# Packed queries and keys made into tiles by masking on ScalarE instead of transfers, with GpSimd and the transfer queue in program order

## The chip, the cores and the metric

The kernel runs on one core of one Trainium2 chip. A core has a matrix engine (TensorE, PE in the profile), three engines for elementwise work (VectorE or DVE, ScalarE or ACT, GpSimd or POOL), a queue that mostly issues transfers (SyncE or SP), and 16 DMA engines which move data between the device memory and the on-chip memory (SBUF). Matrix products land in PSUM[...]. The metric is device time in microseconds (us) of one execution; several runs are taken and their median is given.

## The reference

The input is x, 2 sequences of 2048 tokens with 256 features, in float32. Six blocks are added to it in turn, each on a layer normalization of x:

```python
x = x + 0.5 * L0_ffn(layernorm(x))    # mixture of 6 experts, the best 2 of each token, and a shared one
x = x + L0_attn(layernorm(x))         # 16 heads of 16, every key, q scaled by 1/16
x = x + 0.5 * L0_ffn(layernorm(x))    # the same experts again
x = x + 0.5 * L1_ffn(layernorm(x))    # a gated recurrence of two steps, then a product and tanh
x = x + L1_attn(layernorm(x))         # 16 heads, causal, rotary, relative positions within 32
x = x + 0.5 * L1_ffn(layernorm(x))
```

The first attention is softmax(q k^T) v per head, and an output product with a bias. The second turns q and k by rotary tables (pairs of features, cos and sin of the position), scales q by 1/4, adds to each score the product of q with a learned vector that depends on the distance of key and query, clipped to 32, masks keys that come later, and adds to the weighted values the learned vectors weighted in the same way.

## The kernel before

**Layout and stages.** x stays in SBUF as 32 chunks of 128 tokens; `Norm` (L91 to L120) makes statistics (`stat`, L91/92, DVE), the reciprocal root (`root`, L96 to L98, GpSimd), the normalized tokens (`normal`, L109), and their transposes (`turn`, PE L119, ScalarE L120). By the trace of before, the stages run one after the other: MoE 1 to about 350 us, attention 0 to about 2101, MoE 2 to about 2430, a recurrence to 2628, attention 1 to 3978, and the second recurrence with the output to 4169.

**MoE.** Tokens are sorted by expert into the DRAM buffer `places`, in two halves of 37 tiles of 128 rows. `experts` (L350 to L414) loops over the tiles of one half: load of `xs` (L366), transposes (L369), up product (L376), silu and product (L381, L383), transposes (L388), down product (L395), store to `results` (L402). `combine` (L418 to L428) fetches by GpSimd's indirect transfers (`yg`, L423) the two results of each token of a chunk, and adds them on DVE (L428). The 16 chunks of the second half come at the end of the stage.

**Heads in a tile.** A group is 4 heads at 512 queries. Its queries and keys lie in tiles of 128 partitions, 32 to a head: 16 rows of features, one row in which the keys hold 1 and the queries hold minus the row's maximum, and zeros. A product with a 128-wide piece of the weights gives 128 dense feature rows, that is two groups. ScalarE copies it from PSUM to a tile `packed`, and `spread` brings its rows to the two tiles by eight transfers of 16 rows each on SP's queue. Keys' remaining rows come from a DRAM array `pads` by further transfers (`pad_keys`); queries' tiles are cleared by GpSimd.

**Attention 0** works in units; 16 make a group. In each, PE forms four score products of queries x keys for the maximum (L715, DVE L719), four transposed products (L727), whose exponentials ScalarE takes (L732), and the four weighted sums of the unit before (L739). The result goes through ScalarE (`gather`, L605) to a sum on GpSimd (L610). When a group's maxima are there, `subtract` (L596 to L600) puts their negatives into the queries' tile. Queries are made (L701 to L709) every second group, keys (L680 to L692) and values (L578, L584) of the first sequence before the first unit, those of the second along the way; `divide` (L619 to L623) and `outputs` (L642) end a group and a block.

**Attention 1** has the same pieces under a schedule of steps of two units: for each group n, maxima run in steps `Ms` to `Me`, exponentials in `Es` to `Ee`, and queries come `early`. `rotate` (L961 to L976) does the rotary work: a copy to SBUF (ScalarE), a shuffle (DVE L969) and three operations on GpSimd (L971 to L975). `by_position` (L1019) multiplies queries by the 32 distance vectors; the result is skewed into a diagonal band by a store to DRAM on ScalarE's own queue (`skew<-s`, L1026) and a load (`band_load`, L1036, `band<-skew`, 1.28 MB). `largest` (L1059 to L1097) joins it to the scores (L1083) and finds the maxima, and GpSimd subtracts them from the band (L1097). After use the band goes to DRAM (`band_store`, L1105, `pd<-band`) and comes back by diagonals (`positions_load`, L1182) for the distance vectors' part of the result (`positions_exp`, `positions_T`, `positions`, L1190 to L1201). The schedule is written at L1205 to L1283. Transfers and masks go out in a list `sends`, in half steps.

**Order of work.** Instructions of PE, ScalarE and DVE are issued in program order everywhere (`ENGINES`, L156). SP's, and in the attentions GpSimd's, are placed by a planner, which orders them by its own estimate of times; in MoE and recurrence GpSimd too has program order. Each engine takes its instructions in order, so one that waits holds up those behind it.

```python
def spread(dst, src, i):
    for j in range(J):
        nc.sync.dma_start(out=dst[32 * j : 32 * j + DH], in_=src[ds(64 * i + DH * j, DH), :])
```

Of the kernel before, what the change touches and what calls it, by code (L numbers as in the profile page):

```python
# [10 lines left out]
F32 = mybir.dt.float32  # L11
# [6 lines left out]
P = 128  # L18
# [24 lines left out]
def macaron_kernel(ctx: ExitStack, tc: tile.TileContext, t: dict, out: bass.AP):  # L43
# [8 lines left out]

    xpool = ctx.enter_context(tc.tile_pool(name="xpool", bufs=1))
# [3 lines left out]
    for b in range(NTB):  # L57
        nc.sync.dma_start(out=x[:, ts(b, CPB), :], in_=x_in[:, ts(b, CPB), :])

# [71 lines left out]
    def spread(dst, src, i):  # L131

        for j in range(J):
            nc.sync.dma_start(
                out=dst[32 * j : 32 * j + DH], in_=src[ds(64 * i + DH * j, DH), :]
            )

    def pad_keys(dst):
        n = dst.shape[-1]
        for j in range(J):  # L140
            nc.sync.dma_start(out=dst[32 * j + DH : 32 * j + 32], in_=t["pads"][j, :, 0:n])
# [14 lines left out]
    ENGINES = {mybir.EngineType.PE, mybir.EngineType.Activation, mybir.EngineType.DVE}  # L156
# [9 lines left out]
    def moe(w, ws, gate_w, gate_b, rev, tri, iota, z, behind, last, gathered):  # L166
# [3 lines left out]
        with ExitStack() as s:  # L170
# [179 lines left out]
            def experts(h, exi, between):  # L350

                xT, h_, hT, val = {}, {}, {}, {}
                GROUP = 8

                def tile_in(i):
                    if i % GROUP == 0:
                        n = min(GROUP, NST - i)
                        _, vs = nc.values_load_multi_w_load_instructions(
                            exi[0:1, i : i + n], engines=[mybir.EngineType.PE],
                            min_val=0, max_val=(NE - 1) * EW,  # L360
                            skip_runtime_bounds_check_because="a sum of five comparisons times EW",
                        )
                        for k, v_ in enumerate(vs):
                            val[i + k] = v_
                    xs = wk.tile([P, D], F32, name="xs", bufs=4)
                    nc.sync.dma_start(out=xs, in_=places[h][ts(i, P), :])  # L366
                    pt = bank()
                    for kc in range(2):
                        nc.tensor.transpose(pt[:, ts(kc, P)], xs[:, ts(kc, P)], ident)  # L369
                    xT[i] = wk.tile([P, D], F32, name="xT")  # L370
                    nc.scalar.copy(xT[i], pt[:, 0:D])  # L371

                def up(i):
                    pu = bank()
                    for kc in range(2):
                        nc.tensor.matmul(  # L376
                            pu, lhsT=xT[i][:, ts(kc, P)], rhs=w[:, kc, ds(val[i], 2 * D)],
# [4 lines left out]
                    h_[i] = wk.tile([P, D], F32, name="h")  # L382
                    nc.vector.tensor_tensor(h_[i], sg, pu[:, D:], ALU.mult)  # L383

                def turn(i):
                    ph = bank()
                    for kc in range(2):
                        nc.tensor.transpose(ph[:, ts(kc, P)], h_[i][:, ts(kc, P)], ident)  # L388
                    hT[i] = wk.tile([P, D], F32, name="hT")
                    nc.vector.tensor_copy(hT[i], ph[:, 0:D])  # L390

                def down(i):
                    po = bank()
                    for kc in range(2):
                        nc.tensor.matmul(  # L395
                            po[:, 0:D], lhsT=hT[i][:, ts(kc, P)],
                            rhs=w[:, kc, ds(val[i] + 2 * D, D)],
# [5 lines left out]

                tile_in(0)
                for i in range(NST + 2):
                    between(i)
                    if i + 1 < NST:
                        tile_in(i + 1)
                    if i < NST:
                        up(i)  # L410
                    if 0 <= i - 1 < NST:
                        turn(i - 1)
                    if 0 <= i - 2 < NST:
                        down(i - 2)  # L414
# [17 lines left out]
            def first_half(i):  # L432
                if 3 <= i < 3 + HC:
                    combine(0, i - 3)
# [5 lines left out]
            with tc.manual_schedule(engines={mybir.EngineType.Pool}):  # L440
                stats(0)
                stats(1)
                norm(0)
                stats(2)
                norm(1)
                shared_part(0, 0)
                shared_part(0, 1)
                stats(3)
                norm(2)
                shared_part(0, 2)  # L450
                norm(3)
                shared_part(0, 3)
                mul(0)
                stats(4)
                route(0)
                up(1)
                e0 = sort(0)
                stats(5)
                down(0)
                scatter(0)  # L460
                mul(1)
                up(2)
                stats(6)
                up(3)
                mul(2)
                norm(4)
                norm(5)
                stats(7)
                scatter(1)
                scatter(2)  # L470
                scatter(3)
                down(1)
                mul(3)
                down(2)
                norm(6)
                norm(7)
                down(3)
                route(1)
                up(4)
                mul(4)  # L480
                e1 = sort(1)
                down(4)
                up(5)
                mul(5)
                for b in range(HB, NTB):
                    scatter(b)
                down(5)
                experts(0, e0, lambda i: None)
                experts(1, e1, first_half)
                up(6)  # L490
                mul(6)
                chunks = iter(range(HC))

                def rest(n):
                    for _ in range(n):
                        c = next(chunks, None)
                        if c is not None:
                            combine(1, c)
                            last(c)

                rest(2)
                up(7)
                mul(7)
                rest(1)
                down(6)
                rest(1)
                down(7)
                rest(4)
                if gathered is None:
                    rest(HC)  # L510
            xnT.clear()
            return rest

# [9 lines left out]

    class Pieces:
# [3 lines left out]
        def __init__(self, s, name, norm, weights_o, bias, queries):  # L528
            self.keep = pool(s, name + "_keep")
            self.wk = pool(s, name + "_wk", 2)  # L530
            self.norm, self.wo, self.bias = norm, weights_o, bias
            self.mnegs = []
            for n in range(2):
# [3 lines left out]

            self.qs = [
                self.keep.tile([P, TB], F32, name=f"q{n}") for n in range(queries)
            ]  # L540
            self.cn, self.cT, self.o, self.pTs, self.q = ({} for _ in range(5))

        def clear_queries(self, t):

            for i in range(2):
                self.q[t + i] = self.qs[(t + i) % len(self.qs)]
                nc.gpsimd.memset(self.q[t + i], 0.0)
# [21 lines left out]
        def values(self, v, wv, b, qc, half, row):  # L569

            w = HV * VW
            nc.gpsimd.memset(v[:, :, w:], 0.0)
            dst = v[:, :, 0:w].rearrange("p k (h d) -> p k h d", d=VW)
            nc.gpsimd.memset(dst[:, :, :, DH:], 1.0)
# [10 lines left out]
            else:  # L585
# [4 lines left out]
                )  # L590

# [931 lines left out]
```

## Time and profile before

| what | us |
|---|---|
| median of 3 runs (lowest, highest) | 4171.47 (4168.35, 4172.07) |
| the profiled execution, its span | 4171.17, 4169.4 |
| PE busy in the span (matmul) | 4036.9 (97%) |
| DVE, ACT, POOL busy | 2697.1 (65%), 2498.5 (60%), 1692.5 (41%) |
| mean granted clock of PE | 0.979 |
| attention 0, a window within it (457 to 960): PE busy | 502.60 of 503 |
| attention 1, a window within it (2760 to 2990): PE busy | 219.38 of 230 |

Busy time is the sum over an engine's instructions. PE's matrix products are pipelined and a slower clock makes them longer, so a busy PE can still be slow; the granted clock, as a share of full speed, must be read beside it. A list of waits gives, for each engine, the idle time before its instructions and what ended it. The timeline lists an engine's instructions with start and duration, and the idle time before each in square brackets.

### The profile page before, as it was taken

To read this page: it belongs to the slowest core of one execution; us is meant where nothing else is said; L and a number is where in the kernel's file an instruction comes from. 1 tells how busy PE (TensorE), PEld (TensorE's weight loads), DVE (VectorE), ACT (ScalarE), POOL (GpSimd) and SP (SyncE) were. 2 spreads that over 40 slices of the span, in tenths; PEclk is the share of its full clock that TensorE was granted. 3 is DMA by queue.
4 is the path that set the end of the run, shared out by engine and by line. 5 is a ranking of instruction groups with operands and counts; after the bars stand their busy time and mean duration, and the time that the engine had idled before them with its cause. 6 is when DMAs were issued, how large, how long until landed. Compare 5 with 4: busy or idle time off the path is not lost.

```text
span 4169.4 us, 78015 instructions
## 1 busy us (share of the span) xinstructions
PE 4036.9 (97%) x28256; PEld 1967.4 (47%) x28256; DVE 2697.1 (65%) x6122; ACT 2498.5 (60%) x5091; POOL 1692.5 (41%) x1606
## 2 busy tenths in 40 slices
PE   8997999999999999999999989899999999999999
PEld 4665533333333333333356645555554455555445
DVE  6242888888877788888752444666577666667533
ACT  2331488888877888888933322355557666556832
POOL 4254133336433333333442430445545654544510
PEclk9998899999999999999999999999999999999999
DMA  7343000000000000000043410445433344452101
GB/s 254 119 125 86 15 4 4 4 4 4 4 14 14 4 4 4 4 4 5 9 171 118 127 60 5 106 98 114 95 86 67 81 95 92 86 106 53 45 22 41
DMA packets 376879, 245.34 MB, mean 59 GB/s; under 512 B 157232, under 2 KB 349104, under 8 KB 376496
## 3 DMA queue, kind: packets, MB, share of 16 engines
q1 hardware_dynamic: 298160, 198.39, 18.6%
q0 software_dynamic: 12288, 33.57, 2.5%
q10 hardware_dynamic: 66048, 8.39, 1.4%
q8 instruction: 226, 3.70, 0.4%
q14 instruction: 157, 1.29, 0.1%
HBM read 118.36 MB, written 105.12 MB: 54 GB/s over the span
## 4 chain that ended last, share of the span: by engine, by line
PE 84%; POOL 5%; DVE 4%; DMA 3%; issue 2%; SPq 2%; ACT 1%; ACTq 0%; POOLq 0%; DVEq 0%
PE s L727 13%; PE s L739 12%; PE s L715 10%; PE s L146 8%; PE s L376 6%; PE s L1173 6%; PE s L1059 6%; PE s L1144 5%; PE s L395 3%; DMA band<-skew 2%; PE s L642 1%; POOL places L311 1%; PE s L1154 1%; PE s L1158 1%; PE s L1137 1%
## 5 line engine op out<-in xcount | busy, mean ns | idle before, releaser
L610 POOL TENSOR_TENSOR part<-part 128x512 f32<-128x512 f32 (+3 forms) x800 | 962.6, 1203 | 1407.2 <-ACT part L605 1401.6
L719 DVE TENSOR_REDUCE mx<-s 128x1 f32<-128x512 f32 x2048 | 1270.1, 683 | 331.2 <-PE s L715 331.2
L732 ACT ACTIVATE pT<-s 128x512 f32<-128x512 f32 x2048 | 1063.4, 618 | 239.2 <-PE s L715 237.9
L715 PE MATMUL s<-kT,q 32*128 32x512 f32 x4096 | 1031.9, 630 | 0.0
L727 PE MATMUL s<-q,kT 32*128 32x512 f32 x4096 | 1013.6, 615 | 0.0
L1165 ACT ACTIVATE pT<-s 128x512 f32<-128x512 f32 (+3 forms) x1280 | 588.8, 542 | 223.8 <-PE s L1144 122.3
L605 ACT COPY part<-s 128x512 f32<-128x512 f32 (+3 forms) x864 | 506.5, 587 | 287.9 <-PE s L1173 149.7
L727 PEld LDWEIGHTS s<-q,kT 32*128 32x128 f32 x4096 | 417.9, 184 | 467.2 <-DVE mx L719 326.9
L1067 DVE TENSOR_REDUCE mx<-s 128x1 f32<-128x512 f32 (+1 forms) x768 | 473.3, 679 | 179.5 <-PE s L1059 171.9
L739 PE MATMUL s<-pT,v 128*32 128x512 f32 x4096 | 549.9, 605 | 0.4
L715 PEld LDWEIGHTS s<-kT,q 32*128 32x128 f32 x4096 | 426.4, 187 | 125.5 <-ACT pT L732 77.8
L1059 PE MATMUL s<-kT,q 32*128 32x512 f32 (+7 forms) x2240 | 329.6, 433 | 3.6 <-ACT part L605 3.6
L1173 PE MATMUL s<-pT,v 128*32 128x512 f32 (+3 forms) x2560 | 307.9, 549 | 13.1 <-DVE mx L1083 12.8
L376 PE MATMUL s<-we,xT 128*128 x592 | 279.0, 594 | 0.6 <-ACT xT L371 0.6
L1083 DVE CUSTOM_DVE_ANT_0 band<-s,band 128x160 f32<-128x160 f32 (+1 forms) x512 | 156.1, 316 | 173.2 <-PE s L1059 98.9
L1059 PE MATMUL s<-b,q 32*128 32x512 f32 (+7 forms) x1280 | 246.6, 527 | 13.1 <-ACT part L605 8.6
L383 DVE TENSOR_TENSOR h<-sg,s 128x256 f32<-128x256 f32 x148 | 62.4, 421 | 296.3 <-ACT sg L381 296.3
L739 PEld LDWEIGHTS s<-pT,v 128*32 128x32 f32 x4096 | 82.4, 108 | 335.7 <-ACT pT L732 297.4
L1144 PE MATMUL s<-q,kT 32*128 32x512 f32 (+3 forms) x1152 | 235.5, 509 | 0.0
L423 POOL DMA_INDIRECT yg<-results,at x128 | 125.1, 977 | 232.3 <-DMA results<-y 83.1
L1144 PE MATMUL s<-q,b 32*128 32x512 f32 (+3 forms) x896 | 213.8, 583 | 0.0
L1097 POOL TENSOR_TENSOR band<-band,mneg 128x640 f32<-128x640 f32 x128 | 161.1, 1261 | 97.2 <-DVE mneg L1093 91.4
(207 smaller groups left out, 5159.7 us busy)
## 6 DMA issues: line engine op xcount, KB each, us to landing
band<-skew SPq DMA_DIRECT2D x32, 1280.0 KB
pd<-band SPq DMA_DIRECT2D x32, 1280.0 KB
xs<-places SPq DMA_DIRECT2D x148, 128.0 KB
results<-y SPq DMA_DIRECT2D x148, 128.0 KB
places<-zero SPq DMA_DIRECT2D x2, 4736.0 KB
we<-in_we SPq DMA_DIRECT2D x12, 768.0 KB
skew<-s ACTq DMA_DIRECT2D x32, 256.0 KB
s<-pd SPq DMA_DIRECT2D x32, 256.0 KB
```

What stands on the lines that cost most here:

```text
L376: nc.tensor.matmul(pu, lhsT=xT[i][:, ts(kc, P)], rhs=w[:, kc, ds(val[i], 2 * D)], start=kc == 0, stop=kc == 1,)
L605: nc.scalar.copy(part[:, q0:], pv[:, q0:])
L610: nc.gpsimd.tensor_tensor(o, o, part[:, q0:], ALU.add)
L715: nc.tensor.matmul(ps, lhsT=q[t][rows(j), ts(qb, P)], rhs=kT[b, g][rows(j), ts(kc, TB)], start=True, stop=True,)
L719: nc.vector.tensor_reduce(mx[t][:, qb * J + j, kc : kc + 1], ps, AX.X, ALU.max)
L727: nc.tensor.matmul(st, lhsT=kT[b, g][rows(j), ts(kb, P)], rhs=q[t][rows(j), :], start=True, stop=True,)
L732: nc.scalar.activation(z.pTs[t, kb, j], st, AF.Exp)
L739: nc.tensor.matmul(pv[rows(j), :], lhsT=v[b, g // 2][:, kb, ds(h * VW, 32)], rhs=z.pTs.pop((t, kb, j)), start=True, stop=True,)
L1059: nc.tensor.matmul(ps[:, ds(cols, n)], lhsT=lhsT, rhs=kT[b, c, g][rows(j), ds(k0, n)], start=True, stop=True,)
L1144: nc.tensor.matmul(ps[:, q0:], lhsT=k, rhs=q[t][rows(j), q0:], start=True, stop=True, skip_group_check=True,)
L1165: nc.scalar.activation(z.pTs[t, kb, j][:, q0:], st.pop((t, kb, j))[:, q0:], AF.Exp)
L1173: nc.tensor.matmul(pv[rows(j), q0:], lhsT=v[b, kb // CPB, g // 2][:, kb % CPB, ds(h * VW, 32)], rhs=z.pTs.pop((t, kb, j))[:, q0:], start=T ...
```

## The change

`spread`, `pad_keys`, and the clearing of queries are gone. The columns of the query and key weights are laid out on the host so that one product of 128 columns holds two groups' heads interleaved: for head j of both groups, rows 32j to 32j+15 belong to the first and 32j+16 to 32j+31 to the second. `part_rows` makes each group's tile from it in one operation of ScalarE: every row times 1 or 0 (`rowsel`), plus, for keys, a bias column that puts the 1 into a free row. That row, in which the queries get minus their maximum, is 16 for the first group of a pair and 0 for the second (`row`). Attention 0's factor 1/16 of the queries is now applied to the weights, by a DVE operation at the start of the stage.

SP and GpSimd join the engines in program order. So that GpSimd's operations don't come too soon in it, `later` places its additions one unit after what they add, and the three rotary operations one, two and three units later. In attention 1 queries are made 10 or 8 steps ahead instead of 7, and masked six half steps after; keys, tables and normalization move too; the band's load goes three half steps after `by_position` instead of two, its store four after the end of the maxima instead of three, and `Rs` one step later. The constants in the values' tiles are written once per tile, by ScalarE; the memset in the band is on DVE.

In the MoE the two halves' loops become one of 74 tiles, with `xs` fetched three tiles ahead, and the first half's chunks are combined from the fourth tile of the second half instead of the third. `ws` is loaded before the smaller weights, one half of `places` is cleared before the experts' weights are loaded, and the weights of attention 0 and of the recurrence are loaded there too. `fill_skew`, which writes 32 blocks of constants to DRAM, moves from the start of MoE 2 to step 60 of attention 0.

```diff
-    def spread(dst, src, i):
-        for j in range(J):
-            nc.sync.dma_start(
-                out=dst[32 * j : 32 * j + DH], in_=src[ds(64 * i + DH * j, DH), :]
-            )
-    def pad_keys(dst):
...
+    def part_rows(dst, src, i, bias):
+        nc.scalar.activation(
+            dst, src, AF.Identity, scale=rowsel[:, i : i + 1], bias=0.0 if bias is None else bias
+        )
...
-    ENGINES = {mybir.EngineType.PE, mybir.EngineType.Activation, mybir.EngineType.DVE}
+    E_ = mybir.EngineType
+    ENGINES = {E_.PE, E_.Activation, E_.DVE, E_.Pool, E_.SP}
...
+                for n in range(3):
+                    fetch(n)
                 tile_in(0)
-                for i in range(NST + 2):
-                    between(i)
...
+                for n in range(N + 2):
+                    if n >= NST:
+                        between(n - NST)
+                    if n + 3 < N:
+                        fetch(n + 3)
...
-                if 3 <= i < 3 + HC:
-                    combine(0, i - 3)
+                if 4 <= i < 4 + HC:
+                    combine(0, i - 4)
...
+        def later(self, units, fn, *args):
+            self.due.at(self.unit + units, fn, *args)
+        def begin(self, unit):
+            self.unit = unit
+            self.due.run(unit)
+            self.due.pop(unit, None)
+        def row(self, t):
+            return 0 if t % 2 else DH
...
-            nc.gpsimd.tensor_tensor(o, o, part[:, q0:], ALU.add)
+            self.later(1, nc.gpsimd.tensor_tensor, o, o, part[:, q0:], ALU.add)
...
+            nc.vector.tensor_scalar_mul(wq, wq, 1.0 / 16.0)
...
-                packed = wk.tile([P, TB], F32, name="packed")
-                nc.scalar.copy(packed, pk)
                 for i in range(2):
-                    spread(kT[b, g + i][:, ts(qc, TB)], packed, i)
+                    if qc == 0:
+                        kT[b, g + i] = kpool.tile([P, S], F32, name="kT", bufs=5)
+                    part_rows(kT[b, g + i][:, ts(qc, TB)], pk, i, rowsel[:, 2 + i : 3 + i])
...
+            at(60, fill_skew)
...
-                e = nc.vector if step < 0 else nc.gpsimd
-                e.tensor_tensor(xa, xa, cos[b, qc], ALU.mult)
...
+                    op = nc.gpsimd.tensor_tensor
+                    z.later(1, op, xa, xa, cos[b, qc], ALU.mult)
+                    z.later(2, op, xb, xb, sin[b, qc], ALU.mult)
+                    z.later(3, op, xa, xa, xb, ALU.add)
...
             def queries_out(t):
                 for i in range(2):
-                    spread(q[t + i], packed[t], i)
+                    part_rows(q[t + i], q[t + 1], i, None)
...
-                            nc.gpsimd.memset(band[t][:, 0, :, 0:BAND], MASKED)
+                            nc.vector.memset(band[t][:, 0, :, 0:BAND], MASKED)
...
-                Rs.append(start + 4)
+                Rs.append(start + 5)
...
-                n: max(Ms[n] - 7, Ee[n - 5] + 1) if n > 5 else Ms[n] - 7 for n in range(0, NG, 2)
+                n: max(Ms[n] - 10, Ee[n - 5] + 1) if n > 5 else Ms[n] - 8 for n in range(0, NG, 2)
...
-                sends.at(2 * early[n] + (2 if early[n] < 0 else 3), queries_out, n)
+                sends.at(2 * early[n] + (2 if early[n] < 0 else 6), queries_out, n)
...
-                sends.at(2 * by + 2, band_load, n)
-                sends.at(2 * Me[n] + 3, band_store, n)
+                sends.at(2 * by + 3, band_load, n)
+                sends.at(2 * Me[n] + 4, band_store, n)
```

## The prediction

> **What bounds the kernel.** I read the page's first part, then TensorE's waits, the table of windows, and last the timeline around single waits. TensorE (PE) is busy 4036.9 of a 4169.4 us span, so at most 132.5 us are idle; the rest of any gain must come from clock. The waits of the whole trace, largest first (us in total, times, longest), say where the idle time is:
>
> ```profile
> PE s L578 <- ACT packed L690: 26.0, 6, 6.4
> PE s L119 <- DVE b L109: 15.5, 7, 12.0
> PE s L119 <- DVE xn L109: 12.9, 4, 9.4
> PE s L1173 <- DVE mx L1083: 12.8, 4, 4.1
> PE s L1059 <- ACT part L605: 12.2, 7, 3.1
> PE s L619 <- POOL part L610: 9.4, 7, 2.2
> PE s L1019 <- DVE s L969: 6.3, 1, 6.3
> PE s L1059 <- DMA b<-s: 4.0, 1, 4.0
> ```
>
> The first is the entry to attention 0, the fourth, fifth and last two are attention 1. The windows (length, busy time of PE, PEld, DVE, ACT, POOL, then PE's granted clock) separate the stages:
>
> ```profile
> 457.00:960.00 503.00, 502.60 (x3980) 185.86 (x3980) 417.09 (x693) 413.85 (x805) 191.59 (x157) 1.00 0.02 4
> 2680.00:2760.00 80.00, 76.86 (x697) 42.90 (x696) 48.81 (x152) 46.01 (x100) 43.12 (x40) 0.94 0.55 126
> 2760.00:2990.00 230.00, 219.38 (x1998) 119.60 (x1996) 150.47 (x471) 133.85 (x294) 114.95 (x107) 0.96 0.46 95
> 3300.00:3530.00 230.00, 229.01 (x2080) 126.15 (x2078) 144.90 (x459) 146.51 (x314) 133.18 (x127) 0.99 0.42 91
> 3530.00:3980.00 450.00, 434.51 (x3832) 222.24 (x3830) 283.77 (x821) 296.82 (x633) 214.66 (x195) 0.98 0.37 78
> ```
>
> Attention 0 is full: 502.60 of 503 at clock 1.00. Attention 1 is not: idle time, and a clock below 1. Asked for single stretches there, the windows answer 0.50 nine times, for 57.8 us together, each from the moment of a stall. One such stall in PE's timeline (start, duration, idle before in brackets):
>
> ```profile
> 3540.37 0.66 PE L596 MATMUL s<-ident,mneg 128*128 128x128 f32 x4 [0.29 <-ACT pT L1165]
> 3544.47 1.06 PE L1173 MATMUL s<-pT,v 128*32 128x512 f32 x8 [3.44 <-DVE mx L1083]
> ```
>
> And the timeline of SP's queue before it:
>
> ```profile
> 3529.35 0.38 SPq L1105 DMA_DIRECT2D pd<-band  x1
> 3529.84 1.21 SPq L1036 DMA_DIRECT2D band<-skew  x1
> ```
>
> A 1.28 MB store goes out just before a 1.28 MB load that the next band maximum needs. The load lands 14.14 us later; alone (at 2647) it took 6.62.
>
> [...] the half-speed stretches are 3.4, 6.8 and 10.2 us, though stalls of 1.40 us trigger some too. [...]
>
> **The change, part by part.**
>
> *Entry to attention 0.* Before, each packed key tile is spread by 8 transfers at some 0.6 us per issue, "packed" has two buffers, and the value matmuls wait behind it in PE's order: 26.0 us idle between 371 and 412; the first maximum starts at 416.75. Without transfers that wait goes. But the 1/16 of the queries becomes a DVE multiply on the weights, and in the new order it stands behind the 32 combining operations of MoE 1. These follow POOL's gathers, 1.25 us each from 332.26, so the last is done at about 377.0, and PE, with queries next in order, idles 349.7 to 377.4. Then queries 1.7 (half), keys 13.7, values 8 x 1.87 = 15.0, refilling and half clock after the long idle 3.1 (as after the idle before 2457, where eight transposes took 2.24 instead of 1.04 and the next products 3.55 instead of 1.88), plus the pipeline to the first maximum as before: about 411.2. Gain 5.5. A new 27 us wait takes the place of the old 26; without it the gain would be 32.
>
> *Attention 0, steady.* 0. A unit is 2.93 us of PE; DVE has 2.48, ACT 2.06 + 0.58. Masking is one operation more per query or key tile: (15 + 8) x 0.71 = 16 if ACT were the bound, 0 if the 0.29 us of slack per unit and the buffers absorb it. ACT is busy 413.85 of 503, so I take 0 and keep +16. Where SP waits 1241.9 us for "packed" L706, nobody waits for SP. POOL's remaining blocks of normalization cost PE 5.5 us (L619) in both; taking that away, too, is the lower end.
>
> *MoE.* Merging the halves' expert loops: the five tiles at the seam take 15.94 us against 5 x 3.02 = 15.1, so 0.84 per MoE, 1.7. Earlier loads at the start: PE waits 2.9 for ws, and transfers are bandwidth-bound there, so 0.5 (0 to 2.9).
>
> *MoE 2 to the recurrence.* PE idles 11.98 us before 2457.36 because the reciprocal root stands behind 17 gathers on POOL. In program order it comes after 8 of them, so PE restarts 8 us earlier, at 2449.5. At the third block it must still wait for the last gathers, to about 2481.2 against 2485.8: gain 4.5.
>
> *Start of attention 1.* The waits of 6.29 (L1019) and 3.97 (b<-s) sit on 8 transfer issues, 5.0 us, and their landings between rotation and use. With masking in their place, 5 (0 to 13: the chain through the skew store, 3.85, and band load, 6.62, stays).
>
> *Attention 1, steady.* Two kinds of stall go.
> (i) Six on the queries, 2.78 + 2.69 + 1.40 + 0.59 + 3.11 + 1.40 = 12.0 us. At 2722.03 ACT's queue is held by the skew store (L1026), which waits for a completion counter still owned by a q<-s spread; those spreads wait for POOL's rotation, and exponentials wait behind all of it. No spreads, no wait.
> (ii) Four on the band (L1083), 4.07 + 2.81 + 3.44 + 2.46 = 12.8 us. In program order SP issues the load one unit ahead of the store, and the memset in the band (L1080), on which POOL waited up to 12.4 us, is DVE's.
> (iii) The half-speed stretches after these, 57.8 us, did 28.9 us of full-speed work less; some overlaps the stalls, 25 stays.
> Full value 50. Against it: leads of the band load shrink from 4 units (3.1 us each) to 3 at eleven groups, leaving 9.3 us for a load that takes 6.6 to 14; ACT gets 64 x 0.71 = 45 us more (146.51 of 230 busy in its fullest window); POOL adds come a unit later. I take three quarters: 37 (10 to 50).
>
> Recurrence 2: nothing. fill_skew's 4.6 MB go beside attention 0, whose transfers are at 2%: nothing.
>
> Sum: 5.5 + 0 + 1.7 + 0.5 + 4.5 + 5 + 37 = 54.2. The profiled execution took 4171.17, its span 4169.4, the median of the runs is 4171.47; 4171.2 - 54.2 = **4117**.
>
> **Rivals.** *R1, the gain in attention 1 is mostly given back.* Stalls come from a resource, POOL or transfers, and go elsewhere: 0.59 to 3 us each, with a half-speed stretch behind each. For it: clearing one wait before leaves seven others with the same clock cost, and three-unit leads are short. Against: 3300 to 3530 runs 229.01 of 230 at 0.99 with all these transfers, so steady state can run clean. F then gives 10, the rest the 17.2 above: 4144.
> *R2, everything comes.* F 50, start of attention 1 10, POOL's L619 waits gone 4, MoE start 2.9, DVE's scale not late after all since gathers run ahead +5: 4171 - (10.5 + 4 + 1.7 + 2.9 + 4.5 + 10 + 50) = 4088.
> *R3, slower: ACT waits in order for POOL's rotation.* Before, a transfer queue waited for the rotated tile; now ACT does, in the masking, with the exponentials queued behind it and PE behind those. SP's 257.3 us of waiting for the rotation (POOL s L975, 27 times, up to 29.1) shows that it can be late. It decides if POOL's backlog exceeds the five to six units, some 16 us, between rotation and masking: three rotating operations of 1.27 plus an addition of 1.2 per unit fit in 3.1 each, but a band addition or a normalization burst (4.8) comes on top. At 28 rotations x 3 us late, plus the same again lost at half clock, less the 17 gained elsewhere and the 12.8 of the band: 84 + 84/2 - 30 = +96: 4267; with one in two late, 4204.
> *R4, no change:* transfers were hidden anyway and all gains beyond idle are refilled. Against: the half clock is not hidden behind anything.
>
> **How the numbers follow.** Forecast 0.52 (4100 to 4135 its own range), R1 0.22, R2 0.14, R3 0.08, R4 0.04. R1 and R2 lie on the same side; the range reaches from R2's middle to R1's far end with the attention 0 masking at +16: 4085 to 4162, leaving out R3, R4 and half of R2's upper gain. No change means within 0.2%, 8.3 us, about what a measurement of this kernel can tell: same 0.04, slower 0.08, faster 0.88.
>
> **What would show it.** Right: no waits of PE for "packed"; a single wait of 25 to 28 us of the query product at about 350 for DVE's scaled weights; the first maximum near 411; attention 0 between 457 and 2040 with clock 1.00; the wait before the recurrence cut to about 4 us; no wait on L1083's successor over 1 us, and windows of attention 1 at 0.99. Wrong: ACT in attention 0 waited for by PE every third unit (masking is on the path), ACT waiting for POOL in the masking (R3), band maxima waiting for the band load with the three-unit lead (R1), or skew stores that still hold ACT.

## The result, and the profile after

The changed kernel takes 4120.7 us (median of 4 runs, 4118.86 to 4128.86), the kernel before 4171.77 beside it: a ratio of 0.9882, 95% interval 0.9865 to 0.9900. The profiled execution has a span of 4119.2 us against 4169.4, with a mean granted clock of 0.985 against 0.979. The forecast was 4117 with a range of 4085 to 4162.

The waits of TensorE in the whole trace of the changed kernel (us in total, times, longest):

```profile
PE s L145 <- DVE a_q L721: 35.4, 1, 35.4
PE s L124 <- DVE xn L114: 12.8, 4, 9.3
PE s L657 <- POOL part L541: 8.1, 4, 2.2
PE s L124 <- DVE b L114: 7.4, 6, 3.4
...
PE s L1082 <- ACT q L138: 1.6, 1, 1.6
...
PE s L1236 <- DVE mx L1146: 1.1, 1, 1.1
```

Line numbers are those of the changed kernel. L145 is the products' helper (L146 before), L124 the transposes of normalized tokens (L119), L657 the transposes in `divide` (L619), L1082 the product by position (L1019), L1146 the band maximum (L1083). The 26.0 us behind `packed` are gone and one wait of 35.4 us for the scaled query weights stands in their place. The four band stalls (12.8 us) are down to one of 1.1, the stalls behind ScalarE's held queue (12.2 us at L1059) are out of the list, the wait before the recurrence is 3.4 at the longest instead of 12.0.

Windows over the first and the third quarter of attention 1 (by weighted sums 0 to 640 and 1280 to 1920; length, busy time of PE, PEld, DVE, ACT, POOL, then PE's granted clock), first of the kernel before:

```profile
2686.00:3035.00 349.00, 332.05 (x3050) 182.19 (x3048) 220.95 (x749) 203.36 (x443) 182.30 (x169) 0.95 0.50 107
...
3360.00:3690.00 330.00, 319.90 (x2965) 178.39 (x2963) 202.82 (x686) 203.69 (x443) 175.48 (x163) 0.97 0.46 95
```

The same quarters of the changed kernel:

```profile
2676.00:3002.00 326.00, 321.24 (x3034) 176.18 (x3034) 218.96 (x750) 215.90 (x465) 171.65 (x151) 0.99 0.46 106
...
3324.00:3640.00 316.00, 313.69 (x2963) 173.60 (x2961) 202.27 (x689) 212.87 (x454) 165.46 (x146) 1.00 0.41 93
```

In the first quarter PE's idle time falls from 16.95 to 4.76 us, and its busy time, for the same products, by 10.8; the granted clock rises from 0.95 to 0.99, so that part is clock. In the third it is 10.1 to 2.3, and 6.2. So a bit over half of the gain is idle time and the rest is clock, from the half-speed stretches behind the stalls (57.8 us at 0.50 before), as the prediction had it. ScalarE, which got the masking, is busier by 9 to 13 us in each of these windows and PE's list has hardly a wait for it.

By stage, from the starts of the same instructions in both timelines (differences in us):

```
stage                                              before    after     diff   forecast
start to the last up product of MoE 1              324.50   321.21    -3.3    -1.3
  to the first score product of attention 0         91.10    92.42    +1.3    -5.5
  to the last weighted sum of attention 0         1680.51  1684.84    +4.3     0
  to the last up product of MoE 2                  310.37   311.73    +1.4    -0.8
  to the first product by position                 232.80   222.71   -10.1  } -9.5
  to the first weighted sum of attention 1          46.73    43.01    -3.7  } together
  to the last weighted sum of attention 1         1282.74  1243.28   -39.5   -37
  to the end of the span                           200.64   199.97    -0.7     0
sum                                               4169.39  4119.17   -50.2   -54.2
```

### The profile page after: what moved, and what is told of

It reads as the page before. It is cut to its first block, busy times and chain, and to the rows that moved or that the text cites. A ratio compares the mean times of both kernels' runs of the same rounds, so it can differ in the third digit from the quotient of the medians.

```text
span 4119.2 us, 76457 instructions
## 1 busy us (share of the span) xinstructions
PE 4016.2 (97%) x28256; PEld 1948.3 (47%) x28256; DVE 2703.0 (66%) x6130; ACT 2575.7 (63%) x5227; POOL 1635.1 (40%) x1456
## 4 chain that ended last, share of the span: by engine, by line
PE 89%; DVE 5%; POOL 2%; issue 1%; ACT 1%; DMA 1%; SPq 0%; POOLq 0%; DVEq 0%; ACTq 0%
PE s L771 13%; PE s L783 12%; PE s L757 10%; PE s L145 9%; PE s L1236 6%; PE s L382 6%; PE s L1122 6%; PE s L1207 6%; PE s L402 3%; PE s L680 1%; PE s L1217 1%; PE s L603 1%; PE s L1221 1%; PE s L1200 1%; PE s L930 1%
## 5 line engine op out<-in xcount | busy, mean ns | idle before, releaser
L1146 DVE CUSTOM_DVE_ANT_0 band<-s,band 128x160 f32<-128x160 f32 (+1 forms) x512 | 156.2, 315 | 155.1 <-PE s L1122 75.4
## 6 DMA issues: line engine op xcount, KB each, us to landing
we<-in_we SPq DMA_DIRECT2D x12, 768.0 KB, 11.1
```

## The experiments

Some runs fell on chips where the kernel before takes 4286.49 or 4289.79 us, with longer expert stages (the last up product of MoE 1 comes at 373 to 375 us instead of 321 to 323); ratios are against the kernel before on the same chip, and stages of attention, which last the same there within 3 us, are compared by their traces. "The stretch" below is attention 1 from the first product by position to the last weighted sum: 1329.5 us before, 1286.3 after. Each stretch is read from one trace.

### Entry to attention 0: the scaled weights

```diff
-            nc.vector.tensor_scalar_mul(wq, wq, 1.0 / 16.0)      # start of attention 0
+            ahead.at(2, lambda: nc.vector.tensor_scalar_mul(weights[0], weights[0], 1.0 / 16.0))
             run_moe(n0, ahead.run, nothing, loads0, clear=True)
```

> The changed kernel, with the 1/16 on attention 0's query weights issued on DVE in the MoE, before its last 32 combining operations. Theory (the wait moved from the packed tiles to DVE's order): the 35.4 us idle of PE before the query product goes; queries follow at 346.6, then keys 13.9 and values 14.5 at full clock, so the first score product starts near 377 instead of 413.6. DVE is still held until about 381 by a last combining operation that takes 9.9 us, so the maxima gain 33: about 4088 us (4083 to 4092). Rival (the entry is bound by DVE's and GpSimd's combining anyhow, or by normalized tokens): less than 10 us of gain, over 4111.

Measured: 4088.42 us, ratio 0.9799 (0.9783 to 0.9816). PE's timeline of this run (start, duration):

```profile
346.57 1.88 PE L145 MATMUL s<-b,a_q 128*128 128x512 f32 x4
348.29 13.90 PE L145 MATMUL s<-b,a_k 128*128 128x512 f32 x32
362.02 14.45 PE L603 MATMUL s<-a_v,b 128*128 128x128 f32 x128
376.41 1.14 PE L756 MATMUL s<-kT,q 32*128 32x512 f32 x8
```

PE's timeline of the changed kernel at the same place:

```profile
381.98 3.70 PE L145 MATMUL s<-b,a_q 128*128 128x512 f32 x4 [35.40 <-DVE a_q L721]
385.52 13.90 PE L145 MATMUL s<-b,a_k 128*128 128x512 f32 x32
399.25 14.46 PE L603 MATMUL s<-a_v,b 128*128 128x128 f32 x128
413.63 12.34 PE L757 MATMUL s<-kT,q 32*128 32x512 f32 x47
```

The only edit is where one DVE operation of 0.42 us stands, and the first score product comes 37.2 us earlier. The wait was the order of DVE's instructions. The maxima follow at 381.66, when DVE is through with combining. Half clock cost only the queries here (3.70 us for 1.88, at a granted clock of 0.51 from 381.9 to 385.6): keys and values ran at full length (13.90 and 14.46, clock 1.00), so the refill that the prediction put at 3.1 was 1.8.

Why was the scale done at 381.8 and not at 377? DVE's timeline of the changed kernel:

```profile
369.89 0.48 DVE L440 SCALAR_TENSOR_TENSOR x<-yg,col,x 128x256 f32<-128x256 f32 x1 [0.84 <-DMA yg<-results,at]
371.07 10.43 DVE L440 SCALAR_TENSOR_TENSOR x<-yg,col,x 128x256 f32<-128x256 f32 x2 [0.69 <-DMA yg<-results,at]
381.41 0.42 DVE L721 TENSOR_SCALAR a_q<-a_q 128x512 f32<-128x512 f32 x1
```

and GpSimd's:

```profile
371.46 9.22 POOL L587 TENSOR_TENSOR x<-x,a_b 128x1024 f32<-128x1024 f32 x4
```

One of the two combining operations lasts 9.90 us where the others take 0.48, and it lasts as long as GpSimd adds the bias to the first sequence. Both read two SBUF operands. To see whether GpSimd's additions hold the DVE operation up:

```diff
-                    at(-1, z.add_bias, qc)
+                    at(3 + 4 * qc, z.add_bias, qc)
```

> The changed kernel, with attention 0's bias additions for the first sequence (4 on GpSimd, 2.3 us each, from 371.5 on) moved from before the first unit to steps 3, 7, 11 and 15. Theory: the one combining operation of 9.9 us on DVE is held up by GpSimd, whose bias additions run in the same 9.2 us; without them beside it, it takes 0.5, the weights are scaled near 372.0 instead of 381.8, PE starts 9.8 us earlier: about 4111 (4109 to 4114). Rival (the last gather lands late, and the record of the operation contains its wait): no gain, 4119 to 4122.

Measured: 4117.64 us, ratio 0.9870 (0.9853 to 0.9886), which alone can't be told from the changed kernel's. DVE's timeline of this run:

```profile
371.56 5.81 DVE L440 SCALAR_TENSOR_TENSOR x<-yg,col,x 128x256 f32<-128x256 f32 x2 [0.72 <-DMA yg<-results,at]
377.29 0.42 DVE L721 TENSOR_SCALAR a_q<-a_q 128x512 f32<-128x512 f32 x1
```

GpSimd's:

```profile
371.92 4.63 POOL L587 TENSOR_TENSOR x<-x,a_b 128x1024 f32<-128x1024 f32 x2
```

The edit moved only two of the four additions out of the way: GpSimd has nothing before its first sums of attention 0, so the additions of steps 3 and 7 ran at once. The long DVE operation went from 9.90 us beside 9.22 of GpSimd to 5.29 beside 4.63. So the length follows GpSimd's work, half of it for half: the theory (held up by GpSimd) holds, the expected 9.8 us were not had because the edit was half of one (PE started 4.1 us earlier), and the rival (a late gather) is out, since the gather landed at the same time. The run with SP in program order, below, shows the same with three additions and with one.

Both edits together:

> The changed kernel with both edits: the weights scaled in the MoE, and the bias additions after the first units. Theory: DVE is free at 371.6, PE's first score product comes near 376.7 and sets the entry: gain 37, about 4084 (4079 to 4088); 3 to 5 us better than the first edit alone. Rival: the same as the first edit alone, if DVE is not what the maxima wait for.

Measured: 4082.79 us, ratio 0.9786 (0.9769 to 0.9802), as forecast: 5.6 us better than the first edit alone, and the fastest version of this study, 38 us faster than the changed kernel and some 90 faster than the kernel before.

### Attention 1: what took the stalls away

The prediction gave transfers of queries that hold ScalarE's queue (i), and for the band a store issued just before its load and a memset on GpSimd (ii). First, single parts undone alone. The transfers, put back behind the masking:

```diff
                     part_rows(q[t + i], q[t + 1], i, None)
+                for i in range(2):
+                    for j in range(J):
+                        r_ = q[t + i][ds(32 * j + DH * i, DH)]
+                        nc.sync.dma_start(out=r_, in_=r_)      # and the same for the keys
```

> The changed kernel, with four transfers per group put back in attention 1 behind the masking: each moves 16 rows of the masked query or key tile onto themselves, 32 KB each, as the spreads did, so what uses the tile waits for them. Values and order of everything else stay. Theory (the spreads made the stalls on queries): stalls of 1 to 3 us of PE return in attention 1, waits of the skew store on ScalarE's queue with them, and half-speed stretches: 10 to 30 us slower, 4131 to 4150. Rival (program order of queue and GpSimd with the earlier queries made the gain, transfers are hidden): within 5 us, up to 4126.

Measured: 4129.69 us, ratio 0.9898 (0.9882 to 0.9915). From the recurrence's first gate product to the first weighted sum of attention 1 it takes 244.2 us against 236.8 of the changed kernel, and from there to the last 1243.8 against 1243.3. PE's timeline at the start, of this run:

```profile
2635.40 2.04 PE L1090 MATMUL s<-relk,q 128*128 128x128 f32 x8 [5.50 <-DMA q<-q]
```

and of the changed kernel:

```profile
2632.91 1.16 PE L1082 MATMUL s<-relk,q 128*128 128x128 f32 x8 [1.56 <-ACT q L138]
```

So transfers cost the start of attention 1 some 7 us, where nothing runs beside them, and its steady part nothing. The time lies between the theory's (from 4131) and the rival's (to 4126), but the theory's stalls did not come.

The store half a step earlier, so that it stands ahead of the load again:

```diff
-                sends.at(2 * Me[n] + 4, band_store, n)
+                sends.at(2 * Me[n] + 3, band_store, n)
```

> The changed kernel, with the band's store three half steps after the end of the maxima, as before, instead of four: where a load and a store fall together, the store is issued just ahead of the load. Theory (two band transfers at once delay the load past its use): four stalls of 2.5 to 4 us at the band maxima return, each with a half-speed stretch: 15 to 25 us slower, 4135 to 4146. Rival (lead is enough even with the store ahead, what helped was the masking or the memset): within 4 us, under 4125.

Measured: 4231.89 us, ratio 0.9870 (0.9854 to 0.9887); the stretch takes 1285.0. Seven of the 32 loads now go out right behind a store, as before the change, against none in the changed kernel. The theory is out: with the masks, the earlier queries, GpSimd's order and the memset on DVE in place, that store does no harm.

SP and GpSimd back to the planner in attention 1, with PE, DVE and ScalarE in the same order:

```diff
-    ENGINES = {E_.PE, E_.Activation, E_.DVE, E_.Pool, E_.SP}
+    ENGINES = {E_.PE, E_.Activation, E_.DVE}      # all stages but attention 1 keep Pool and SP in order
```

> The changed kernel, with SP's and GpSimd's instructions of attention 1 placed by the planner again (20 of SP's 452 rows and some 49 of GpSimd's 615 move; PE, DVE and ScalarE keep their order). Theory (masking makes most of attention 1's 39.5 us, order the band's part of about 20): 10 to 25 us slower, 4131 to 4146. Rival 1 (order is all of it): 35 to 40 slower, about 4158. Rival 2 (masking is all of it): within 4 us.

Measured: 4228.68 us, ratio 0.9862 (0.9845 to 0.9878); the stretch takes 1286.1. Program order is not needed either. (In the four runs with the planner in attention 1, GpSimd's bias additions also come earlier, at a time when DVE isn't combining; no combining operation is long in them, and the entry to attention 0 takes 84.3 to 86.1 us against 92.4 of the changed kernel. So the stretch is what can be compared, not the whole time.) And the queries' lead alone:

```diff
-                n: max(Ms[n] - 10, Ee[n - 5] + 1) if n > 5 else Ms[n] - 8 for n in range(0, NG, 2)
+                n: max(Ms[n] - 7, Ee[n - 5] + 1) if n > 5 else Ms[n] - 7 for n in range(0, NG, 2)
```

> The changed kernel with queries 7 steps ahead instead of 10 or 8, and nothing else: masks, program order and later sends stay, so by_position and the band's load come with less lead. Theory B (lead is the cause): 1300 us or more in the stretch that takes 1286 now. Theory A (waiting transfers are the cause): 1284 to 1292.

Measured: 4232.87 us, ratio 0.9866 (0.9850 to 0.9883); the stretch takes 1284.4. Four single steps back, and none brings the steady part's stalls back. So they were undone together. First transfers straight from the rotated tile, which make SP wait for GpSimd as before, and the planner. This kernel leaves out the masking of queries, so the other group's rows are not zero in its tiles; the next one does too.

```diff
                 for i in range(2):
-                    part_rows(q[t + i], q[t + 1], i, None)
+                    for j in range(J):
+                        nc.sync.dma_start(out=q[t + i][rows(j)], in_=q[t + 1][rows(j)])
```

> The changed kernel with two things of attention 1 undone together: the query tiles are made by four transfers per group straight from the rotated tile (so SP's queue waits for GpSimd, as before; the other group's rows are not masked out, which leaves the masking of queries out), and SP and GpSimd are placed by the planner there. Queries stay early. From the first product by position to the last weighted sum the changed kernel takes 1286 us, the kernel before 1329. Theory A (a transfer that waits for GpSimd holds the skew store, whatever the lead): 1305 or more. Theory B (the earlier queries alone give the rotation its time, so neither transfers nor order matter): 1284 to 1292.

Measured: 4228.44 us, ratio 0.9855 (0.9839 to 0.9872); the stretch takes 1284.3. With early queries not even both matter: theory A is out. And with late queries as well (the line for `early` shown last, and their transfers four half steps after instead of six), and the memset on GpSimd again:

```diff
-                sends.at(2 * early[n] + (2 if early[n] < 0 else 6), queries_out, n)
+                sends.at(2 * early[n] + (2 if early[n] < 0 else 4), queries_out, n)
-                            nc.vector.memset(band[t][:, 0, :, 0:BAND], MASKED)
+                            nc.gpsimd.memset(band[t][:, 0, :, 0:BAND], MASKED)
```

> As the run with transfers and planner, and besides queries 7 steps ahead instead of 10 or 8, their transfers four half steps after instead of six, and the memset in the band on GpSimd: all of attention 1's query path as before, but for the keys' masking. Theory A and B both: the stretch takes 1315 to 1330 us instead of 1286, the stalls of 1 to 3 us at queries and bands are back with their half-speed stretches. Rival C (the keys' transfers are what crowds the queue): below 1300.

Measured: 4260.55 us, ratio 0.9932 (0.9915 to 0.9948); the stretch takes 1314.1, 1 us short of the lower bound expected. Both kinds of stall are back. ScalarE's timeline of this run, with its queue's issues (ACTq):

```profile
2817.19 0.58 ACT L1088 COPY s<-s 128x512 f32<-128x512 f32 x1 [0.25 <-PE s L1083]
2821.19 0.40 ACTq L1090 DMA_DIRECT2D skew<-s  x1
2821.68 0.58 ACT L643 COPY part<-s 128x512 f32<-128x512 f32 x1 [3.91 <-DMA q<-q]
```

and PE's:

```profile
2822.32 0.40 PE L1123 MATMUL s<-b,q 32*128 32x32 f32 x2 [1.94 <-ACT part L643]
...
2979.64 1.11 PE L634 MATMUL s<-ident,mneg 128*128 128x128 f32 x4 [3.15 <-DVE mx L1147]
```

This is the picture of the prediction (in the trace of before, the copy of a partial sum at 2722.52 is idle for 4.70 us until a `q<-s` transfer has landed): the copy for the skew store ends at 2817.77, the store is issued at 2821.19, after a query transfer's landing, and the copy of a partial sum behind it on ScalarE, for which PE waits, is 3.91 us late. The second line is the other kind, behind a band maximum.

The last run parts the two kinds. It has masks in place of the queries' transfers and is the same in all else.

```diff
-                    for j in range(J):
-                        nc.sync.dma_start(out=q[t + i][rows(j)], in_=q[t + 1][rows(j)])
+                    part_rows(q[t + i], q[t + 1], i, None)
```

> As the run with transfers, planner, late queries and the memset on GpSimd (1314 us from the first product by position to the last weighted sum), but with the queries' masking by ScalarE in place of their transfers: SP's other transfers keep their order. Theory (two kinds of stall with two causes): the stalls on products by position behind ScalarE's held queue, 1.94 + 1.35 + 1.81 + 1.40 us there, go with the transfers, and the stalls on the band maxima, 3.15 + 3.9 + 1.49, stay, with their half-speed stretches: 1298 to 1306 us. Rival 1 (the transfers' share of bandwidth also delays the band loads): all stalls go, 1284 to 1290. Rival 2 (order and lead make all stalls): 1310 to 1316.

Measured: 4130.62 us, ratio 0.9904 (0.9888 to 0.9921); the stretch takes 1297.4, 0.6 below what was expected. PE's timeline of this run around one of its stalls:

```profile
2856.09 0.66 PE L634 MATMUL s<-ident,mneg 128*128 128x128 f32 x4 [1.31 <-DVE mx L1146]
2862.20 0.66 PE L657 MATMUL s<-ident,part 128*128 128x128 f32 x4 [2.43 <-POOL part L541]
```

The stalls behind ScalarE's held queue are gone. Those behind the band maxima stay (four, 0.56 to 1.89 us), and each is followed by one behind GpSimd's sums (0.82 to 2.44); at each, 3.4 us run at half clock. GpSimd's list of waits in this run has the memset in the band:

```profile
POOL band L1143 <- DMA band<-skew: 51.1, 6, 12.1
```

At each of the four stalls GpSimd stands idle 10.8 to 12.1 us in this memset until the band's load has landed, and its sums queue up behind it; before the change it was 11.8 to 12.4 us at the four band stalls. With the memset on DVE and the planner kept (two of the runs above), no wait behind a band maximum exceeds 1.3 us. So for this kind the memset is a likely cause; it was not undone alone. With late queries and the planner, then, 16.7 us of the stretch hang on the query transfers (1314.1 to 1297.4) and 11.1 on what remains, order, lead, the timing of the masking and the memset together (1297.4 to 1286.3). Another 15.4, from 1329.5 to 1314.1, separate the fullest undoing from the kernel before: it still has masked keys and the later sends and sums. Which of these makes them was not tried.

### Program order for SP without the rest

```diff
-    ENGINES = {mybir.EngineType.PE, mybir.EngineType.Activation, mybir.EngineType.DVE}
+    ENGINES = {mybir.EngineType.PE, mybir.EngineType.Activation, mybir.EngineType.DVE, mybir.EngineType.SP}
```

> The kernel before, with SP alone added to the engines in program order, so that all its spreads stay. Theory (order alone can't help while spreads wait at the head of SP's queue for GpSimd's rotation or for packed tiles): not faster by more than 5 us than before, likelier slower by 5 to 40 us, since a waiting spread now holds the band's loads behind it: 4167 to 4212. Rival (order alone brings the band's gain): faster by 15 to 25, about 4150.

Measured: 4939.18 us, ratio 1.1521 (1.1501 to 1.1541). In PE's list of waits of this run one line stands out:

```profile
PE s L369 <- DMA xs<-places: 455.3, 134, 19.4
```

and in SP's:

```profile
SPq L402 <- ACT y L401: 1061.7, 147, 53.4
```

The direction was right, the place and the size were not. In the expert loop the load of a tile is written behind the store of an earlier tile's result, which waits for ScalarE; in program order every load waits with it, and both MoE stages take about twice as long. The stretch of attention 1 takes 1313.2, 16.2 less than before: there the order alone helps, as the rival had it, with all transfers of queries and keys, the late queries and the memset in place. No wait behind a band maximum L1083 is left, and of the 12.2 us behind ScalarE's held queue this:

```profile
PE s L1059 <- ACT part L605: 0.6, 1, 0.6
```

So SP's order alone ends both kinds of stall. Other waits, of 12.6, 10.3 and 9.8 us, take part of their place.

In this run GpSimd's bias additions come between gathers, three together and then one. DVE's timeline, and GpSimd's:

```profile
708.08 7.92 DVE L428 SCALAR_TENSOR_TENSOR x<-yg,col,x 128x256 f32<-128x256 f32 x1 [0.70 <-DMA yg<-results,at]
708.75 6.96 POOL L560 TENSOR_TENSOR x<-x,a_b 128x1024 f32<-128x1024 f32 x3
```

Beside the single addition of 2.35 us, a combining operation takes 3.30.

### The loads at the start

```diff
-            gate_w, ws, gate_b, rev, tri, iota = (
+            gate_w, gate_b, rev, tri, iota, ws = (
...
-            clear_places(0)
...
+            clear_places(0)
             clear_places(1)
```

> The changed kernel, with the loads at the start of the MoE in the old order: the shared weights after the five small ones, and both halves of the sorted buffer cleared after the experts' weights. Theory: the 2.5 us by which the first expert product came earlier are lost, 4123 (4122 to 4125). Rival (they come from GpSimd's program order in the sorting): no change, 4120 to 4121.

Measured: 4231.11 us, ratio 0.9865 (0.9849 to 0.9882). On the same chip, the first expert product comes at 117.75 us against 115.76 in the run with the earlier store, whose MoE is that of the changed kernel, and the first score product at 469.41 against 467.62. That is 1.8 to 2.0 us later, but the planner run on this chip, with the loads in the new order, has its first expert product at 118.54, and in the changed kernel's own trace and in five others with expert stages as short it lies between 98.8 and 100.3. In the whole time no loss shows. What the order of loads is worth is not shown.

## Why the prediction was right

The sum, 54.2, came out at 50.2, and its largest term was sized within 7%. That the whole is so near is in part luck: the entry to attention 0 missed by 6.8 us, attention 0 by 4.3 and MoE 2 by 2.2 to the one side, MoE 1 by 2.0, the stretch before attention 1 by 4.3, attention 1 by 2.5 and the end by 0.7 to the other. Step by step:

**Entry to attention 0: mechanism right, 6.8 us off.** The prediction named the new wait, its cause and its place (one wait of 25 to 28 us at about 350 for DVE's scaled weights). It was 35.4. MoE 1 ended 3.1 us earlier, which only lengthens the wait, and the scale ended 4.4 us later than worked out. The term that was mis-sized is the end of the combining operations, "the last is done at about 377.0", where it ended before. Two things move it, and in part they cancel. The last gather is issued at 369.57 instead of 373.04, so that the last combining operation would end near 372.8 (an estimate: 2.7 us of landing as for the gathers before it, and 0.48). But program order puts GpSimd's four bias additions next to the gathers and makes the operation before the last 9.90 instead of 0.48. The prediction moved GpSimd's gathers on paper but did not ask what GpSimd does right after them and whether DVE feels it. The first two experiments show both parts. The terms also add to more than was written: 377.4 with 1.7, 13.7, 15.0 and 3.1 is 410.9, and with the 1.15 us from the first score product to the first maximum 412.0, not 411.2.

**Attention 0, steady: +4.3 where 0 was taken and +16 kept.** A masking operation here takes 0.684 us for queries and 0.773 for keys. The prediction took 0.71 for both, which was the author's estimate. An exponential, with no operand for each partition, takes 0.618, a gate of the recurrence, with a bias for each partition, 0.687. A query mask has one such operand (`rowsel`), a key mask two, and the plain copy's 0.59, 0.684 and 0.773 lie 0.09 apart. Table loads are 15 in both traces, 1.28 us each. PE stays nearly full (599.41 of 600 in a window where before it had 600.00). Of the 4.3 us, some 1.6 come at one place: PE waits 1.99 us for GpSimd's sum at 971, where before it waited 1.75, and now 3.4 us at half clock follow. In nine further traces with masking the stage takes 1683.2 to 1683.4 us and in one 1684.9, in both without it 1680.4 and 1680.5. (The run with the scale in the MoE is left aside: its first score products wait for their maxima.) So the stage as changed costs about 3 us; that the masking makes them is likely, but was not tried by itself.

**MoE: -3.3 and +1.4 where -1.3 and -0.8 stood.** The seam of the halves gave 0.8 us per MoE, as worked out. The start gave 2.5 instead of 0.5, inside its bounds; what makes it is open (the wait for `ws` is 2.3 us instead of 2.9, and the DMA engines' mean busy share in the first 20 us is 0.96 where before it was 0.95). MoE 2 lost 2.2 us at its start, with a clock of 0.83 in the window from 2098 to 2108 where before it was 1.00; what tipped it was not tried.

**The recurrence and the start of attention 1: -13.8 where -9.5 stood.** PE restarts 8.4 us earlier after the normalization, counted from the first gate product (14.05 against 22.45 us), where 8 was said; 5.9 of it are left at the recurrence's last output product, where 4.5 was said. From there to the first weighted sum 8.5 us are gained where 5 stood, of which putting transfers back takes about 7.4 away again: the 5 taken for these issues and landings was low.

**Attention 1: -39.5 where -37 stood, but not for the reason given in full.** The jumps between the two timelines lie at the stalls named (6.6 us at 2723, 8.0 at 2945, 5.1 at 2985, 8.0 at 3298, 5.1 at 3643 in the time of before, and the four at the band). What each stall is, the runs with transfers, planner and late queries show, and that the two kinds are separate, the last of them shows. But the prediction said "No spreads, no wait", and of the band that the load is now ahead of the store, each as if it were needed. Neither is: with the queries 10 steps ahead and the memset on DVE, transfers, store order and planner do nothing, alone or two together; with the masks and program order, late queries do nothing; and in the kernel before, SP's order alone ends both kinds in its trace. The stalls came back when late queries and the memset on GpSimd were put back in one step on top of the planner and the transfers. These two were not parted. By the schedule the band's load goes out at the same step with late and with early queries, so for the band the memset, which the prediction had named, fits better than the lead. The prediction read lead only as something that shrinks ("from 4 units to 3"), and overlooked that the lead of the queries grows. How much of this term each part would carry alone in the kernel before is shown for SP's order only.

**The rivals.** R1 (new small stalls give most back) did not come: the clock in attention 1 is 0.99 to 1.00. R3 (ScalarE waiting for the rotation) did not: for the masking from a rotated query tile, ScalarE is idle 4.0 us in all, 32 operations. R2's "DVE's scale not late" was the opposite of what happened, and is what the edited version then brought. What the prediction left out, and the run with SP alone in order shows, is that program order on SP depends on fetching expert tiles three ahead: that part of the change was booked as nothing, and without it the order costs hundreds of us.

## What to carry to other kernels

When an edit moves one operation to an in-order engine, look up what stands ahead of it there: 0.42 us of scaling behind 32 combining operations cost 35 us of waiting, and issuing it earlier gave 32 back. Before crediting one part of a change with a stall's end, undo the parts together as well as singly: here SP's order ended the stalls without masks or early queries, and early queries with the memset on DVE did so without masks for the queries or order, so each looked worthless when undone alone. And a queue put in program order needs its loads written ahead of the stores that wait: where they stood behind, PE waited 455.3 us for them.

## What the runs showed of the hardware that had not been expected

A DVE operation with two SBUF inputs, the combining (`x<-yg,col,x`), lasted until GpSimd's additions with two SBUF inputs (`x<-x,a_b`) beside it had ended. It takes 0.48 us alone. Beside one addition it took 3.30 us, beside two 5.29 and 5.41, beside three 7.92, beside four 9.87 to 9.92 (six traces), and each time its record ends 0.29 us after that of GpSimd's last addition. The four additions are separate instructions of 2.34 us each, and the record of the one combining operation spans them all; it shows no wait, only a long duration. What makes it so long was not measured. DVE additions with one input in PSUM and one in SBUF (`x<-s,x`, 0.69 us) last as long beside GpSimd's operations with two SBUF inputs (9 cases in the attentions of the changed kernel's trace) as without. Two SBUF tensors are not needed for it, though: the normalization's operation (`b<-x,mv,rstd`), with one SBUF tensor and 0.41 us alone, took 1.10 to 1.43 us in five cases where a GpSimd addition began before it or with it, and ended 0.15 us after that addition.
